# Layer 2's weight product in seven-product form, with the adjacency products between the weight products

## The chip, the cores and the metric

The kernel runs on one core of a Trainium2 chip. The metric is the device time of one execution in microseconds; the kernel before takes 1877.01 us in the median of 3 runs (1876.96 to 1878.04). Everything is computed in float32.

The engines of the core work through their own instruction streams in order and wait for each other by semaphores: TensorE (PE in the profile; PEld is its loading of the stationary operand), VectorE (DVE), ScalarE (ACT), GpSimd (POOL) and SyncE (SP), which issues most DMAs.

## What is computed

Four residual layers act on x of shape 128 x 64 x 256 (8192 rows of 256). Each takes `h = relu(layernorm(x))` and adds a graph layer of h: layer 0 two graph convolutions and four LSTM variants, layer 1 a graph convolution with two batch norms, layer 2 a product with three parts of the adjacency, layer 3 causal attention inside each graph of 64 rows. The change is in layer 2:

```python
adj_0 = jnp.diag(jnp.diagonal(adj))
adj_1 = jnp.triu(adj, k=1)
adj_2 = jnp.tril(adj, k=-1)
h = jnp.einsum('bjf,kfo->kbjo', x, W)        # W is 3 x 256 x 256
out = adj_0 @ h[0] + adj_1 @ h[1] + adj_2 @ h[2]    # per graph, then + bias
```

The last line is shortened. The kernel takes the products in the other order: first the three adjacency parts with the input, then the three weight matrices, summed.

## The kernel before

Rows are worked on in 16 supertiles of 512 rows (four quarters `q` of 128). Layers 0 and 1 come first. What matters here is the last stage, which runs from 1450 us to the end: it holds the end of layer 1, layer 2 and layer 3, in eight pairs of supertiles, an even one (`s` = 0, 2, ...) and an odd one. For each supertile, in `rest`:

- `load` fetches the residual x1 by DMA; `affine` (L1200) scales the batch-normed product of layer 1, which lies feature-major, on VectorE (on ScalarE for s = 1); `turn` (L1215) transposes it on TensorE and `turned` (L1223) adds x1 from PSUM: x2.
- `norm` (L1226) of x2 gives h2: `stats` per quarter on VectorE, `root` adds epsilon on VectorE (L1240) and takes the power -1/2 on GpSimd (L1241), `shift` makes the negative mean times root on VectorE (L1244), and `relu` (L1248) runs on ScalarE, one instruction per quarter. `biased` (L1261) adds layer 2's bias to x2 on GpSimd.
- `graphs3` (L1263) multiplies with the three adjacency parts. Each graph has 64 rows, so the stationary operand is 64 x 128, and two graphs use the two row halves of the array (64*128 in the profile). It is called four times, for each chunk `c` of 128 features and each half `k` of the rows. A call has four products and fills two PSUM banks, one copied out by ScalarE and one by VectorE (L1278), into `ag`.
- `weigh` (L1280) multiplies with the weights: for each quarter six products (two chunks by three adjacency parts), with `ag` stationary and 256 weight columns moving, 24 a supertile. `weighed` (L1288) adds x2 and gives x3.
- `norm` of x3 gives h3, which is transposed (`h3`, L1298) and copied (L1302). The attention follows: a query-key product in seven-product form (`qsum` L1313 makes the data sums on VectorE, `qproduct` L1326), the value product `hv` (L1350), `scores` (L1360), mask, maximum, exponentials on ScalarE, `turn_e` (L1381) with its copy (L1385), and `attend` (L1391), whose result is added on VectorE (L1396) and stored by DMA.

The order of the work is written by hand. Each step is put into a list with a planned time (`at(t, fn, ...)`, relative to `PERIOD * i` for pair i), the list is sorted (L1483), and each engine gets its instructions in that order. The times are only a sorting key: nothing waits for them. All PSUM banks of this stage, eight of them, come from one pool, `bank()`; a tile waits until the one that held its bank has been read. The seven-product form (Strassen's in Winograd's variant) splits both operands in 2 x 2 blocks and needs seven block products instead of eight, with sums of blocks prepared on both sides and results added up afterwards. `OF` and `weight_sum` hold its bookkeeping for the stages that already use it.

In pair i, steps of three pairs overlap: the turns and the normalization of the next pair, the weight products and queries of this one, and the last steps of the attention of the odd supertile before. The lines that set this are

```python
rest(2 * i, at, i, -8.6 if first_ else -40.2, -38.3, 0, (7.0, 12.6), 29.0, ...)
at(t_G + 0.8 * k, graphs3, ...)
at(t_W[k] + 2.6 * q, weigh, k, q)
```

where the even supertile is turned 40.2 and the odd one 27.6 before their pair's origin, and the adjacency products of the odd supertile start 3.5 after those of the even one, so that the two stand next to each other on TensorE.

Of the kernel before, what the change touches and what calls it, by code (L numbers as in the profile page):

```python
# [9 lines left out]
F32 = mybir.dt.float32  # L10
AF = mybir.ActivationFunctionType
# [9 lines left out]
def kernel(ctx: ExitStack, tc: tile.TileContext, a: dict, out: bass.AP):  # L21
# [85 lines left out]
    eps = const.tile([P, 1], F32, tag="eps", name="eps")  # L107
# [771 lines left out]
    def bn_coeffs(name, co, stats, c):  # L879
# [6 lines left out]
        nc.gpsimd.tensor_add(v, mv[:, 1:2], eps)  # L886
# [11 lines left out]
    with tc.tile_pool(name="pz", bufs=1, reuse_waits="tile") as pz:  # L898
# [238 lines left out]
        wl2 = [weight(f"wl2_{k}", a["W"][k], late) for k in range(3)]  # L1137
# [6 lines left out]

        with tc.tile_pool(name="tp", bufs=2, reuse_waits="tile") as tp_:
            tp.append(tp_)
            emit(1e9)
# [31 lines left out]

    PERIOD, HALF = 52.5, SUP // 2  # L1180
    NP = NS // 2
    with tc.tile_pool(name="pc", bufs=2, reuse_waits="tile") as pc, \
# [3 lines left out]
        def rest(s, at, only_pair, t_T, t_n, t_G, t_W, t_h, t_QH, t_S, t_soft, t_E, t_O, end):  # L1186
# [13 lines left out]
            def affine(c):  # L1200
                if s == 1:
                    nc.scalar.activation(y[c], y[c], AF.Identity, bias=co2[:, 1, c : c + 1],
                                         scale=co2[:, 0, c : c + 1])
                    return
                nc.vector.tensor_scalar(y[c], y[c], co2[:, 0, c : c + 1], co2[:, 1, c : c + 1],
                                        op0=ALU.mult, op1=ALU.add)
# [19 lines left out]
            def norm(src, tag, halves, t_rows, t_relu):  # L1226
# [11 lines left out]
                def root(qs):  # L1238
                    rn = v["rn"][:, 0, qs]
                    nc.vector.tensor_scalar_add(rn, v["mv"][:, qs, 1], EPS)  # L1240
                    nc.gpsimd.tensor_tensor(rn, rn, mhalf[:, : qs.stop - qs.start], ALU.pow)  # L1241

                def shift(qs):
                    nc.vector.scalar_tensor_tensor(v["rn"][:, 1, qs], v["mv"][:, qs, 0], -1.0,  # L1244
                                                   v["rn"][:, 0, qs], op0=ALU.mult, op1=ALU.mult)
# [5 lines left out]
                at(t_rows[0] - 0.01, new)  # L1251
                for q in range(Q):
                    at(t_rows[q // 2] + 0.6 * (q % 2), stats, q)
                for k, qs in enumerate((q2s(0), q2s(1)) if halves else (slice(0, Q),)):
                    at(t_relu[k] - 1.5, root, qs)
                    at(t_relu[k] - 0.1, shift, qs)
# [23 lines left out]
            def weigh(k, q):  # L1280
                if q == 0:
                    v["W"] = two(bank())
                for n in range(3 * KC):
                    c, m = divmod(n, 3)
                    nc.tensor.matmul(v["W"][:, q, :], v["ag"][:, c, m, ts(2 * k + q, P)],  # L1285
                                     wl2[m][:, c, :], start=(n == 0), stop=(n == 3 * KC - 1))

            def weighed(k):  # L1288
                if k == 0:
# [234 lines left out]
```

## Time and profile before

| quantity | value |
|---|---|
| median of 3 runs | 1877.01 us |
| the profiled execution | 1876.78 us, of which the span is 1875.1 us |
| granted TensorE clock | 1.00 |
| TensorE busy, whole span | 1853.9 us (99%) |
| one pair of the last stage (start to start of its adjacency products) | 50.88 us |
| engines busy from 1492 to 1545 us: DVE, ACT, POOL | 38.6, 21.4, 10.1 us |

A line of the profile in order of time reads: start, duration, engine, source line, operation, output<-inputs, shape, count. Numbers in brackets say how long the engine was idle before and what ended the wait. Instructions that follow each other are merged into one line with a count. A float32 product gives two records on TensorE. Ends of TensorE records are modelled and overlap the next start, so its rates are read from start to start. In the page's groups, a line holds the source line, the operation, shapes and count, then the busy time, the mean of one in ns, and the idle time before.

### The profile page before, as it was taken

How to read it: one execution, taken by the hardware profiler on the slowest of the kernel's cores; microseconds unless marked ns; L12 is line 12 of the kernel's file. 1: busy time of each engine (PE TensorE's matmuls, PEld its weight loads, DVE VectorE, ACT ScalarE, POOL GpSimd, SP SyncE). 2: the span in 40 equal slices, each digit the busy share in tenths (PEclk: the TensorE clock that was granted, in tenths of full speed). 3: DMA queues.
4: the chain of work that ended last, by engine and by line, in shares of the span. 5: the costliest groups of instructions: out<-in, count | busy, mean ns of one | idle time of the engine just before them, and what ended most of it. 6: DMA issues, size and time to landing. Idle time of an engine off the chain costs nothing.

```text
span 1875.1 us, 19841 instructions
## 1 busy us (share of the span) xinstructions
PE 1853.9 (99%) x7080; PEld 1168.8 (62%) x7080; DVE 1129.4 (60%) x2254; ACT 925.7 (49%) x1594; POOL 645.4 (34%) x553
## 2 busy tenths in 40 slices
PE   8999999999999999999999999999999999999999
PEld 7997444444445666666444444566444788888887
DVE  6775777634546435445633333588876776667674
ACT  6776666534435334433533333378685434433442
POOL 4451422443424433422442222267353412211220
PEclk9999999999999999999999999999999999999999
DMA  4110001000001000000000000243200111111101
GB/s 146 57 57 1 1 1 29 16 1 0 1 0 45 1 0 1 1 1 1 23 0 0 1 0 0 102 132 116 71 1 2 44 46 46 35 46 46 46 23 34
DMA packets 50642, 54.86 MB, mean 29 GB/s; under 512 B 3184, under 2 KB 45936, under 8 KB 50544
## 3 DMA queue, kind: packets, MB, share of 16 engines
q1 hardware_dynamic: 50096, 53.30, 8.9%
q8 instruction: 56, 0.92, 0.2%
q14 instruction: 42, 0.34, 0.1%
q10 hardware_dynamic: 448, 0.30, 0.0%
HBM read 36.55 MB, written 17.04 MB: 29 GB/s over the span
## 4 chain that ended last, share of the span: by engine, by line
PE 93%; DVE 3%; POOL 1%; ACT 1%; DMA 1%; issue 1%; SPq 0%; ACTq 0%; DVEq 0%; POOLq 0%
PE ps L686 34%; PE ps L692 19%; PE ps L1285 8%; PE ps L930 5%; PE ps L1047 4%; PE ps L1350 3%; PE ps L392 3%; PE ps L402 3%; PE ps L1326 2%; PE ps L431 2%; PE ps L1273 2%; PE ps L1360 2%; PE ps L1391 1%; PE ps L623 1%; PE ps L1298 1%; PE ps L579 1%
## 5 line engine op out<-in xcount | busy, mean ns | idle before, releaser
L708 DVE TENSOR_TENSOR gate<-gate,ps 128x512 f32<-128x512 f32 (+2 forms) x378 | 223.9, 620 | 449.0 <-PE ps L692 367.7
L686 PE MATMUL ps<-tx,wih 128*128 128x512 f32 (+2 forms) x996 | 441.2, 541 | 1.9 <-ACT gate L711 1.0
L686 PE MATMUL ps<-hT,wih 128*128 128x512 f32 (+2 forms) x756 | 338.5, 541 | 0.0
L711 ACT COPY gate<-ps 128x512 f32<-128x512 f32 (+2 forms) x252 | 134.5, 534 | 378.4 <-PE ps L692 325.4
L686 PEld LDWEIGHTS ps<-tx,wih 128*128 128x128 f32 x996 | 188.4, 190 | 188.2 <-issue 128.2
L704 ACT ACTIVATE gate<-gate,lbias 128x512 f32<-128x512 f32 (+2 forms) x252 | 216.7, 860 | 160.0 <-DVE gate L708 160.0
L692 PE MATMUL ps<-h,whh 128*128 128x512 f32 (+2 forms) x576 | 256.6, 527 | 0.0
L686 PEld LDWEIGHTS ps<-hT,wih 128*128 128x128 f32 x756 | 143.6, 190 | 141.6 <-issue 79.4
L692 PE MATMUL ps<-th,whh 128*128 128x512 f32 (+2 forms) x432 | 192.5, 527 | 0.0
L731 POOL TENSOR_TENSOR gate<-gate 128x1024 f32<-128x1024 f32 (+2 forms) x36 | 71.9, 2019 | 297.5 <-ACT gate L704 297.5
L1285 PE MATMUL ps<-wl,ag 128*128 128x256 f32 x768 | 172.1, 380 | 0.0
L692 PEld LDWEIGHTS ps<-h,whh 128*128 128x128 f32 x576 | 109.4, 190 | 100.2 <-issue 76.5
L1285 PEld LDWEIGHTS ps<-wl,ag 128*128 128x128 f32 x768 | 143.4, 190 | 20.2 <-ACT ag L1278 1.8
L731 POOL TENSOR_TENSOR cell<-gate 128x1024 f32<-128x1024 f32 (+2 forms) x36 | 79.4, 2225 | 174.8 <-ACT gate L704 174.8
L1241 POOL TENSOR_TENSOR ln_rn<-ln_rn,mhalf 128x4 f32<-128x4 f32 (+1 forms) x33 | 32.8, 995 | 300.8 <-DVE ln_rn L1240 300.3
L692 PEld LDWEIGHTS ps<-th,whh 128*128 128x128 f32 x432 | 82.1, 190 | 75.2 <-issue 57.4
L1248 ACT ACTIVATE h<-x,ln_rn 128x256 f32<-128x256 f32 x128 | 68.2, 593 | 103.3 <-DVE ln_rn L1244 103.3
L731 POOL TENSOR_TENSOR cell<-gate,cell 128x1024 f32<-128x1024 f32 (+2 forms) x31 | 62.8, 2044 | 110.2 <-ACT gate L704 110.2
L711 DVE COPY gate<-ps 128x512 f32<-128x512 f32 (+2 forms) x126 | 78.6, 624 | 20.8 <-PE ps L692 20.8
L704 ACT ACTIVATE gate<-ps,lbias 128x512 f32<-128x512 f32 (+2 forms) x126 | 79.6, 631 | 3.8 <-PE ps L692 1.0
L736 ACT ACTIVATE gate<-cell 128x1024 f32<-128x1024 f32 (+2 forms) x72 | 68.0, 951 | 26.1 <-POOL cell L731 26.1
L648 DVE TENSOR_TENSOR tx<-hT,tx 128x512 f32<-128x512 f32 (+2 forms) x70 | 57.7, 825 | 13.8 <-PE ps L686 10.2
(236 smaller groups left out, 2933.8 us busy)
## 6 DMA issues: line engine op xcount, KB each, us to landing
xt<-in_x_dram SPq DMA_DIRECT2D x30, 512.0 KB, 4.2
x1d<-xt SPq DMA_DIRECT2D x16, 512.0 KB, 3.0
x<-x1d SPq DMA_DIRECT2D x16, 512.0 KB, 4.9
out_dram<-x SPq DMA_DIRECT2D x15, 512.0 KB, 3.0
wih<-in_WihT_dram SPq DMA_DIRECT2D x16, 256.0 KB, 4.8
whh<-in_WhhT_dram SPq DMA_DIRECT2D x12, 256.0 KB, 4.8
xt<-in_x_dram SPq DMA_DIRECT2D x6, 128.0 KB, 3.2
wl<-in_W_dram SPq DMA_DIRECT2D x3, 256.0 KB, 3.6
```

The lines of the kernel that those rows point to most:

```text
L648: yield nc.vector.tensor_sub(t[k], *((b[1][0], b[0][0]), (b[1][1], t[0]), (b[1][1], b[1][0]), (b[0][1], t[1 % len(t)]))[k])
L686: nc.tensor.matmul(wide(p_[:, :N]), wih[0][:, OF[k], gi, :], x_, start=first_, stop=(j == 0), skip_group_check=True)
L692: nc.tensor.matmul(p_[:, :N], whh[0][:, OF[k], gi, :], h_, start=False, stop=True, skip_group_check=True)
L704: nc.scalar.activation(to, r[bank_][:, :N] if bank_ else to, fn, bias=lbias[:, l, m : m + 1])
L708: nc.vector.tensor_add(slot(n, hc), slot(n, hc), r[bank_][:, :N])
L711: op(slot(n, hc), r[bank_][:, :N])
L731: fn(*((t["G"] if isinstance(t, dict) and "G" in t else st["c"])[:, n, :, : st["N"]] for t in tiles))
L736: nc.scalar.activation(o_, c, AF.Tanh)
L930: nc.tensor.matmul(r[name], con["w1"][:, OF[j], g, :], x_, start=new, stop=(name, j) in (("a", 4), ("b", 3), ("c", 2)), skip_group_check=True)
L1047: nc.tensor.matmul(banks[name], w2[:, OF[j], k, :], x_, start=(new and k == 0), stop=(k == 1), skip_group_check=True)
L1248: nc.scalar.activation(v[tag][:, q, :], v[src][:, q, :], AF.Relu, bias=v["rn"][:, 1, q : q + 1], scale=v["rn"][:, 0, q : q + 1])
L1285: nc.tensor.matmul(v["W"][:, q, :], v["ag"][:, c, m, ts(2 * k + q, P)], wl2[m][:, c, :], start=(n == 0), stop=(n == 3 * KC - 1))
```

## The change

- Layer 2's weight product goes to the seven-product form for every supertile but the first. The blocks are two chunks of 128 features by two halves of 256 rows on the data side, and 2 x 2 blocks of 128 x 128 on the weight side, each for three adjacency parts. `ag` and its sums stay the stationary operand; 128 columns of weights or of weight sums move. A product of the form (`gproduct`) has six matmuls, two for the 128-row parts by three adjacency parts; seven of them are 42 a supertile. Data sums (`gsum`) are four GpSimd operations over 128 x 3 x 256; the weight sums are made once, on GpSimd. Results leave PSUM by seven VectorE operations (`gevict`, `gadd`) over 128 x 256. Supertile 0 uses the eight-product form with 128 moving columns (`gdirect`, 48 matmuls).
- The PSUM banks of the stage are split into three pools: one bank for the accumulation called "a", two for "b" and "c", five for all other tiles. The query products use the first two pools as well.
- The epsilon addition, the power and the shift of `root` run on GpSimd, now four operations. `qsum` moves from VectorE to GpSimd. `affine` moves to ScalarE for all supertiles but the first.
- The order changes. The even supertile is turned 14.5 before its pair's origin (40.2 before), the odd one 6.05 (27.6 before), with normalization and ReLU after that. The odd supertile's four `graphs3` calls, 1.3 apart from 7.9 on, stand between the even supertile's weight products. The seven data products of a supertile are 1.3 apart.
- The tiles of the sums and of `qk` reuse buffers of weights that are no longer needed.

```diff
-        wl2 = [weight(f"wl2_{k}", a["W"][k], late) for k in range(3)]
+        wl2 = late.tile([P, 7, 3, P], F32, tag="wl2", name="wl2")
+        for o in range(2):
+            for c in range(2):
+                nc.sync.dma_start(wl2[:, 2 * o + c], a["W"].rearrange(
+                    "m (c p) (o n) -> o c p m n", c=2, o=2)[o, c])
...
+        for k in range(4):
+            if k != 2:
+                at(B + 60 + 5.16 * k, weight_sum, wl2, k)
...
+    new_banks(a=1, bc=2, psum=5)
...
             def affine(c):
-                if s == 1:
-                    nc.scalar.activation(y[c], y[c], AF.Identity, bias=co2[:, 1, c : c + 1],
-                                         scale=co2[:, 0, c : c + 1])
+                if first_:
+                    nc.vector.tensor_scalar(y[c], y[c], co2[:, 0, c : c + 1], co2[:, 1, c : c + 1],
+                                            op0=ALU.mult, op1=ALU.add)
                     return
-                nc.vector.tensor_scalar(y[c], y[c], co2[:, 0, c : c + 1], co2[:, 1, c : c + 1],
-                                        op0=ALU.mult, op1=ALU.add)
+                nc.scalar.activation(y[c], y[c], AF.Identity, bias=co2[:, 1, c : c + 1],
+                                     scale=co2[:, 0, c : c + 1])
...
                 def root(qs):
-                    rn = v["rn"][:, 0, qs]
-                    nc.vector.tensor_scalar_add(rn, v["mv"][:, qs, 1], EPS)
-                    nc.gpsimd.tensor_tensor(rn, rn, mhalf[:, : qs.stop - qs.start], ALU.pow)
-
-                def shift(qs):
-                    nc.vector.scalar_tensor_tensor(v["rn"][:, 1, qs], v["mv"][:, qs, 0], -1.0,
-                                                   v["rn"][:, 0, qs], op0=ALU.mult, op1=ALU.mult)
+                    rn, nm = v["rn"][:, 0, qs], v["rn"][:, 1, qs]
+                    n = qs.stop - qs.start
+                    nc.gpsimd.tensor_add(rn, v["mv"][:, qs, 1], eps[:, :n])
+                    nc.gpsimd.tensor_tensor(rn, rn, mhalf[:, :n], ALU.pow)
+                    nc.gpsimd.tensor_mul(nm, v["mv"][:, qs, 0], rn)
+                    nc.gpsimd.tensor_mul(nm, nm, mone[:, :n])
...
-            def weigh(k, q):
+            def gsum(k):
+                if k == 0:
+                    v["t2"] = late.tile([P, 3 * KC, D], F32, tag="wT", name="tg")
+                t1, t2 = v["t2"][:, 0:3], v["t2"][:, 3:6]
+                if k == 0:
+                    nc.gpsimd.tensor_sub(t1, g_(0, 1), g_(0, 0))
+                elif k == 1:
+                    nc.gpsimd.tensor_sub(g_(0, 1), g_(1, 1), g_(0, 1))
+                elif k == 2:
+                    nc.gpsimd.tensor_add(t2, g_(0, 1), g_(0, 0))
+                else:
+                    nc.gpsimd.tensor_sub(g_(1, 0), g_(1, 0), t2)
+
+            def gproduct(name, j):
+                new = ("g", name) not in v
+                if new:
+                    v["g", name] = two(bank("a" if name == "a" else "bc")[:, :HALF])
...
+                for p_ in range(2):
+                    for m in range(3):
+                        nc.tensor.matmul(v["g", name][:, p_, :], x_[:, m, ts(p_, P)], wl2[:, OF[j], m, :],
+                                         start=new and p_ == m == 0,
+                                         stop=m == 2 and (name, j) in (("a", 4), ("b", 3), ("c", 2)),
+                                         skip_group_check=True)
...
-                nc.vector.tensor_add(v["x3"][:, q2s(k)], v["x2"][:, q2s(k)], v["W"])
+                nc.vector.tensor_add(w_("x3", o, n), w_("x2", o, n), v["g", name])
+
+            def gadd(o, n, name):
+                nc.vector.tensor_add(w_("x3", o, n), w_("x3", o, n), v["g", name])
...
-                nc.vector.tensor_sub(t[:, k], *(None, (b_(0, 1), b_(0, 0)), (b_(1, 1), t[:, 1]),
+                nc.gpsimd.tensor_sub(t[:, k], *(None, (b_(0, 1), b_(0, 0)), (b_(1, 1), t[:, 1]),
...
+                for t, (name, j) in zip(t_W, (("c", 2), ("a", 1), ("b", 5), ("a", 6), ("b", 3), ("a", 7), ("a", 4))):
+                    at(t, gproduct, name, j)
...
+                for t, fn, *args in ((0, gevict, 0, 0, "c"), (1, gadd, 0, 0, "a"), (2, gevict, 1, 1, "b"), (3, gevict, 0, 1, "a"),
+                                     (6, gevict, 1, 0, "a"), (4, gadd, 0, 1, "b"), (5, gadd, 1, 1, "a")):
+                    at(t_W[t] + 1.35, fn, *args)
...
-            rest(2 * i, at, i, -8.6 if first_ else -40.2, -38.3, 0, (7.0, 12.6), 29.0, 32.6, 40.0, 42.7,
+            rest(2 * i, at, i, -8.6 if first_ else -14.5, -12.5, 0,
+                 (7.0, 9.6, 12.2, 14.8) if first_ else (7.0, 8.3, 9.6, 10.9, 12.2, 13.5, 16.8),
+                 (3.3, 5.2, 7.1, 9.0), (12.5, 17.5) if first_ else (18.3, 15.3), 21.3, 24.6, 31.4, 40.0, 42.7,
...
-            rest(2 * i + 1, at, i, -3.0 if first_ else -27.6, 1.5 if first_ else -25.4, 12.3 if first_ else 3.5, (17.8, 26.5), 39.1,
+            rest(2 * i + 1, at, i, -3.0 if first_ else -6.05, 1.5 if first_ else -5.2,
+                 12.25 if first_ else 7.9, (17.85, 19.6, 20.9, 22.2, 23.5, 24.8, 27.5),
+                 (16.0, 17.9, 18.1, 22.0) if first_ else (12.3, 14.2, 16.1, 22.0), (31.4, 30.6), 35.3, 39.1,
```

## The prediction

> **What bounds the kernel now.** I read the page's busy table first, then TensorE alone in order of time, then all engines over one pair of supertiles.
>
> ```profile
> PE 1853.9 (99%) x7080; PEld 1168.8 (62%) x7080; DVE 1129.4 (60%) x2254; ACT 925.7 (49%) x1594; POOL 645.4 (34%) x553
> L1285 PE MATMUL ps<-wl,ag 128*128 128x256 f32 x768 | 172.1, 380 | 0.0
> ```
>
> TensorE is busy 99% of the span. The second line is the product that the change rewrites: 768 records are 16 supertiles of 24 products, two records to an f32 product. A busy share can hide waits, so I take TensorE from start to start, in the view in order of time:
>
> ```profile
> 1509.18 1.95 PE L1360 MATMUL ps<-h3T,qk 128*128 128x128 f32 x16
> 1510.96 1.89 PE L1391 MATMUL ps<-hw,eT 128*128 128x256 f32 x8
> 1512.79 5.47 PE L1273 MATMUL ps<-adj,h 64*128 64x192 f32 x64
> 1518.19 5.45 PE L1285 MATMUL ps<-wl,ag 128*128 128x256 f32 x24
> 1523.47 0.60 PE L1381 MATMUL ps<-ident,sc 128*128 128x128 f32 x4
> ...
> 1829.21 10.53 PE L1285 MATMUL ps<-wl,ag 128*128 128x256 f32 x48
> 1839.57 1.89 PE L1391 MATMUL ps<-hw,eT 128*128 128x256 f32 x8
> ```
>
> 48 records of 256 columns take 10.36 us: 0.216 each. 16 records of 128 columns, each with its own stationary, take 1.78: 0.111 each. The 64 adjacency records (L1273; two 64-row tiles side by side) take 5.40. ScalarE's copies of their groups of eight start every 0.65 us, which is 0.081 a record and 5.20 for 64. The excess sits at the edges: the eight L1391 records before them take 1.83 where 8 x 0.216 is 1.73, the last adjacency record runs out 0.20 late, and the 24 records after them take 5.28 where 24 x 0.216 is 5.18. **One block of adjacency products costs 0.40 us at its two edges.** L1273 starts again at 1563.67, 1614.55, and on to 1818.09, always 50.88 apart. My sum of one pair from these rates is 50.68; the other 0.2 is a wait for ReLU before L1298. So the pair has almost no slack in TensorE, and the order of its instructions decides what else may show.
>
> The other engines' durations come from the same view of all engines:
>
> ```profile
> 1564.62 0.48 ACT L1278 COPY ag<-ps 128x384 f32<-128x384 f32 x1 [4.21 <-PE ps L1273]
> 1576.26 1.28 DVE L1224 TENSOR_TENSOR x<-x,ps 128x512 f32<-128x512 f32 x2
> 1577.45 0.42 DVE L1235 BATCH_NORM_STATS2 ln_st<-x 128x6 f32<-128x256 f32 x1
> ...
> 1581.84 1.02 POOL L1241 TENSOR_TENSOR ln_rn<-ln_rn,mhalf 128x4 f32<-128x4 f32 x1 [26.78 <-DVE ln_rn L1240]
> 1582.89 0.16 DVE L1244 SCALAR_TENSOR_TENSOR ln_rn<-ln_mv,ln_rn 128x4 f32<-128x4 f32 x1 [0.60 <-POOL ln_rn L1241]
> ...
> 1583.09 2.08 ACT L1248 ACTIVATE h<-x,ln_rn 128x256 f32<-128x256 f32 x4 [10.58 <-DVE ln_rn L1244]
> ```
>
> Eviction 0.60 from start to start, statistics 0.53 per quarter, power 1.02, four ReLUs 2.08, adjacency copy 0.48. VectorE starts 0.2 after TensorE's end, a copy of L1273 0.27.
>
> **What the Trainium skill says.** "TensorEngine Tiling (Array Packing)", Key Properties: changing the tiling mode drains TensorE; the 0.40 us a block agrees. "TensorE: Matmul & The Clock Gate", Back-to-back issue gap and LDWEIGHTS: the spacing in a stream is set by the weight load and the matmul together, the load by its columns. The trace agrees that a load of 128 columns still hides behind 128 moving columns (0.111 against half of 0.216). "GPSIMD Engine Reference", Key points: GpSimd contends with VectorE instructions that read two SBUF tensors. Here L1313 took 0.42 alone and 0.94 beside L1261. "Perfetto Trace Analysis" on GpSimd says to trust spacing rather than spans, so for its small operations I take the spacing of the chain L888, L889, L890: 0.27.
>
> **The change, part by part, for a steady pair.**
>
> 1. Weight product: 24 x 2 x 0.216 = 10.36 becomes 42 x 2 x 0.111 = 9.33 per supertile: -1.03, over 15 supertiles -15.4. Supertile 0 goes direct in 48 products of 128 columns: 10.66, +0.3.
>
> 2. Adjacency products between weight products: before, the 64 records of a pair are one block. In the changed order the even supertile's 32 are a block and the odd one's four groups of eight are each a block between weight products: five blocks, four more edges, +1.6 a pair in pairs 1 to 7, +11.2. Pair 0 has three blocks in both. The gain of 1 is 2.06 a pair, so 0.46 remains.
>
> 3. Turns, normalization and ReLU of the next pair, which stood up to 40 us ahead of its adjacency products, now stand just before them. This is the step that I expect to hurt. Count from the end of the odd supertile's last turn transpose. TensorE runs on: three products 1.30, score transposes 0.44, scores 1.78, attention 1.73, edge 0.10, two adjacency groups 1.30: it wants the third group of the even supertile at 6.65. VectorE: start 0.2, second eviction done near 1.0, three statistics 1.6, the copy of the score transposes (0.7, ahead of the fourth in VectorE's order), the fourth 0.53 and its tail: 3.94. GpSimd: a hop of 0.12, add 0.27, power 1.09, two multiplies 0.46: 5.88. ScalarE's order is odd ReLU, ReLU, ReLU, then the even supertile's first adjacency copy. Three ReLUs from 5.95 end at 7.42, the copy at 7.90. The third group needs the bank that this copy frees, for only five banks are left to everything but the products (one pool of eight before). So it starts at 7.95; the fourth needs the second copy, which stands behind the fourth ReLU: 8.82, end 9.47, against 7.95 unhindered. **Stall 1.5 us a pair, 7 pairs: +10.5.** A place, not a rate: it is there only if the chain is late by more than the reach. Below nothing it can't go; if the hops are shorter than I read it is 1.0, if VectorE is held up 2.2.
>
> 4. One bank for the accumulation "a": each eviction must read it before the next product of "a" may add. Between the sixth and seventh product of the even supertile only 0.44 of transposes lie, against 0.2 + 0.42 + 0.05 for VectorE's add: +0.23 a pair. The other waits of this kind have 1.3 us of cover. Pair 0 has none in this place: +0.65.
>
> 5. Data sums on GpSimd, four of 128x768 per supertile. The trace has no such row; it has these:
>
> ```profile
> L731 POOL TENSOR_TENSOR gate<-gate 128x1024 f32<-128x1024 f32 x20 | 46.6, 2351 | 184.3 <-ACT gate L704 184.3
> L423 POOL TENSOR_TENSOR t<-g 128x256 f32<-128x256 f32 x30 | 21.9, 731 | 71.3 <-ACT g L396 71.3
> ```
>
> A line through them gives 1.81 at 768 (bounds 1.5, of two 128x384 passes without start cost, and 2.35). Eight make 14.5 a pair; with query sums (8 x 0.73), bias (8 x 0.74), and four roots (4 x 1.82) GpSimd has 33.5 of 52 us, from 11. On the path: in the frame of 3 the first sum starts at 9.0 behind the biases, the third ends at 14.6, TensorE asks for it near 17. The odd third ends at 24.9, needed at 28. Hidden with 2 to 3 us to spare; without that cover each late microsecond counts whole.
>
> 6. Off VectorE: scaling (0.53 each, 0.80 on ScalarE, issued 17 us early), query sums, root add and shift. Seven evictions of 0.42 replace two of 0.68. VectorE goes from 37.5 to about 32 us a pair and loses its contending operations: nothing on the path. The root on GpSimd alone is 1.82 against 0.17 + 1.02 + 0.16 with hops, about +0.3 in each chain, already in step 3. Before the odd h3 transposes the chain (evict, attention, statistics 2.1, root 1.8, ReLU 2.1) is 8.4 against 8.3 of TensorE: +0.1 where 0.2 was. In the last pair no turn fills in: +0.9.
>
> 7. Pair 0: its wait of 0.8 for L1302 goes, one of about 1.2 for GpSimd's crowded roots (weight sums, biases) comes; with its own 1.0 from step 1, 0.3 lost on supertile 0, 0.65 from step 4, 0.5 for banks at the start, and 1.8 of idle there unchanged, my walk through its order ends 0.8 early. Four loads of weights instead of three, and three GpSimd weight sums of about 1 us in the stage before, have tens of us until use: nothing.
>
> Sum: pair 0 -0.8; pairs 1 to 6 each -2.06 + 1.6 + 1.5 + 0.23 - 0.1 = +1.2, +7.0; pair 7 -2.06 + 1.6 + 1.5 + 0.23 + 0.9 = +2.2. Together +8.4 on the profiled 1876.78 (span 1875.1, 1.7 outside it), which is 0.2 under the median 1877.01: **1885**.
>
> **Rivals.** *The ReLU chain arrives in time* (not slower): step 3 vanishes if the odd ReLU starts 1.5 us earlier than my sum has it; a bit less than half of it must vanish for the slowdown to fall under 0.2%. For it: 1.3 us of eight small operations with hops are my reading. Against: every duration is a row of the trace. 1885 - 10.5 = 1874.5.
> *Edges cost nothing beside short products as well* (faster): with both 10.5 and 11.2 gone, 1863. Against it: three blocks of different length show the same 0.4.
> *GpSimd becomes the bound*: above about 2.3 us per 768-wide sum its cover is gone and the root behind the odd sums holds h3; one us a pair, 1892.
> *The product doesn't shrink*: loads of 128 columns showing beside 128 moving ones would give 42 x 2 x 0.19 = 16.0 by the load's own span, +11 a pair; the 0.111 of L1360 rules it out.
>
> **How the numbers follow.** No change means within 0.2%, 3.75 us, about what a measurement can tell. My case has 0.50 (1881 to 1890), GpSimd 0.13, the chain in time 0.20 (1871 to 1879), both gone 0.17. Slower 0.50 + 0.13 + 0.02, same 0.16, faster 0.17 + 0.02. From 1869 to 1892 leaves 0.13 below and 0.06 above.
>
> **What would show it.** In the changed trace: weight products of 128 columns at 0.111 from start to start; four short adjacency blocks between them, each with 0.4 of edges; a TensorE gap of 1 to 2 us inside the even supertile's 32 adjacency records, released by ScalarE's copy; pairs 52 us apart; GpSimd near 33 us of a pair, 768-wide sums near 1.8. Pairs under 50.5 apart would make me wrong.

## The result and the profile after

The changed kernel takes 1888.39 us in the median of four runs (1887.98 to 1889.16), the kernel before 1876.99 us beside it (1876.65 to 1878.04): a ratio of 1.006, 95% interval 1.0043 to 1.0078. It is slower by 11.4 us. The prediction said 1885.0 us (1869 to 1892), with 0.65 for slower. The profiled execution took 1887.99 us, its span 1886.2 us, 11.1 more than before, at the same granted clock of 1.00.

The page's busy table and the group of the rewritten product (engine, busy time, share, instructions; then line, shapes, count, busy, mean ns of one, idle before):

```profile
PE 1857.4 (98%) x7668; PEld 1176.9 (62%) x7668; DVE 1094.8 (58%) x2175; ACT 943.9 (50%) x1622; POOL 815.9 (43%) x777
L1314 PE MATMUL ps<-wl,ag 128*128 128x128 f32 x900 | 111.9, 278 | 1.9 <-POOL ag L1300 1.2
```

TensorE's share fell from 99% to 98%, although it has more instructions: it waits now. Products are named below by their number in the form; in order of time a supertile's seven are the second, first, fifth, sixth, third, seventh and fourth, of which the first, sixth, seventh and fourth go to the accumulation "a". Where TensorE waits is seen in the view of TensorE in order of time over one pair (start, duration, line, tiles, shape, count; in brackets the idle time before and its releaser):

```profile
1618.07 1.57 PE L1281 MATMUL ps<-adj,h 64*128 64x192 f32 x16
1620.53 1.79 PE L1281 MATMUL ps<-adj,h 64*128 64x192 f32 x16 [0.89 <-ACT ag L1286]
1622.25 1.60 PE L1314 MATMUL ps<-wl,ag 128*128 128x128 f32 x12
1623.78 0.92 PE L1281 MATMUL ps<-adj,h 64*128 64x192 f32 x8
1624.63 1.60 PE L1314 MATMUL ps<-wl,ag 128*128 128x128 f32 x12
...
1634.57 0.60 PE L1432 MATMUL ps<-ident,sc 128*128 128x128 f32 x4
1635.34 4.25 PE L1314 MATMUL ps<-wl,ag 128*128 128x128 f32 x36 [0.17 <-POOL ag L1300]
1639.43 2.84 PE L1314 MATMUL ps<-wl,tg 128*128 128x128 f32 x24
1642.11 1.50 PE L1314 MATMUL ps<-wl,ag 128*128 128x128 f32 x12
...
1670.31 1.57 PE L1281 MATMUL ps<-adj,h 64*128 64x192 f32 x16
```

Pairs are 52.24 apart (1618.07 to 1670.31), 50.88 before: +1.36. From start to start: the even supertile's 32 adjacency records take 4.18 (1618.07 to 1622.25). Four groups at 0.65 and the 0.20 at the end are 2.80, so 1.38 is a wait: 1.16 where the third group begins (1619.37 to 1620.53), 0.22 behind it. A product of the form takes 1.53 between two adjacency blocks (1622.25 to 1623.78) and 1.34 elsewhere (1642.11 to 1643.45); a block of eight records takes 0.85 where 0.65 would be eight of 0.081. That is 0.20 in the block and 0.20 in the products beside it, 0.40 a block. The score transposes (1634.57) take 0.77 to the next start where four take 0.44: 0.33 of wait.

The span's 11.1 us, from the starts of the adjacency blocks: pair 0 begins 0.58 earlier (1460.88 against 1461.46) and lasts 52.70 against 51.33, +0.8 in sum; six pairs of +1.36 are +8.2; from the last pair's start to the end it is 59.17 against 57.01, +2.2.

Below, "apart" is always the distance between two pairs' adjacency blocks in the steady part.

### The profile page after: what moved, and what is told of

Same layout as the page of the kernel before. It is cut to its first block, busy times and chain, and to the rows that moved or that the text cites. A ratio compares the mean times of both kernels' runs of the same rounds, so it can differ in the third digit from the quotient of the medians.

```text
span 1886.2 us, 21316 instructions
## 1 busy us (share of the span) xinstructions
PE 1857.4 (98%) x7668; PEld 1176.9 (62%) x7668; DVE 1094.8 (58%) x2175; ACT 943.9 (50%) x1622; POOL 815.9 (43%) x777
## 4 chain that ended last, share of the span: by engine, by line
PE 85%; POOL 7%; DVE 4%; ACT 2%; issue 1%; DMA 0%; POOLq 0%; DVEq 0%; ACTq 0%
PE ps L688 34%; PE ps L694 19%; PE ps L932 5%; PE ps L1049 4%; PE ps L1314 4%; PE ps L394 3%; PE ps L404 3%; PE ps L1401 2%; PE ps L433 2%; PE ps L1377 2%; POOL ag L1300 1%; PE ps L625 1%; POOL tg L1298 1%; ACT h L1257 1%; PE ps L1411 1%
## 5 line engine op out<-in xcount | busy, mean ns | idle before, releaser
L1314 PE MATMUL ps<-wl,ag 128*128 128x128 f32 x900 | 111.9, 278 | 1.9 <-POOL ag L1300 1.2
L1314 PEld LDWEIGHTS ps<-wl,ag 128*128 128x128 f32 x900 | 104.7, 192 | 9.3 <-issue 5.4
L1286 DVE COPY ag<-ps 128x384 f32<-128x384 f32 x64 | 35.5, 555 | 57.7 <-PE ps L1281 57.4
L1381 ACT COPY qk<-ps 128x256 f32<-128x256 f32 x60 | 22.1, 369 | 88.5 <-PE ps L1377 69.3
```

What stands on the lines that cost most here:

```text
L1314: nc.tensor.matmul(v["g", name][:, p_, :], x_[:, m, ts(p_, P)], wl2[:, OF[j], m, :], start=new and p_ == m == 0, stop=m == 2 and (name, j) ...
```

## The experiments

The theory in the prediction: the product gains 2.06 a pair on TensorE, and three things take back more than that, the edges of adjacency blocks (1.6), the late normalization chain in front of them (1.5), and a single bank for the accumulation "a" (0.23). The rivals: too few banks, GpSimd at its bound, or a product that doesn't gain. The first four runs take these apart one at a time, the next four ask what else can take their place, and the last four try to collect the gain. Four of the twelve expectations were met (the late ReLUs, the one block, the exchanged products, and pair 0 in the part that its edit touches). Most misses have one form: a cost was gone as expected, and another wait stood in its place.

### The odd ReLUs behind the even adjacency copies

```diff
-t_n + (4.1 if s == 1 else 3.8 if s % 2 else 7.5)
+t_n + (4.1 if s == 1 else 7.9 if s % 2 else 7.5)
```

> The odd supertile's four ReLUs stand behind the even supertile's four adjacency copies on ScalarE; nothing else of the chain is shortened. My theory: the 1.4 us gap inside the even supertile's adjacency products comes from the first copy standing behind three late ReLUs, so the gap nearly goes, and the first odd adjacency group waits about 0.3 us instead: about 1.0 less a pair, 7 pairs, 1881 us (1879 to 1884), pairs about 51.2 apart. Rival, too few PSUM banks: the third group has to wait for a copy whatever stands before it, the gap keeps 1 us or more, 1887 to 1889.

Measured: 1882.93 us, ratio 1.0031 (1.0019 to 1.0042). Pairs are 51.44 apart, 0.80 less than in the changed kernel. What changed is ScalarE's order. ScalarE in the changed kernel:

```profile
1618.53 1.58 ACT L1257 ACTIVATE h<-x,ln_rn 128x256 f32<-128x256 f32 x3 [2.83 <-POOL ln_rn L1254]
1620.02 0.46 ACT L1286 COPY ag<-ps 128x384 f32<-128x384 f32 x1
1620.38 0.60 ACT L1257 ACTIVATE h<-x,ln_rn 128x256 f32<-128x256 f32 x1
```

Three ReLUs that wait for GpSimd's root, then the copy of the first adjacency group, which TensorE has finished near 1618.8, then the third group at 1620.53. With the edit, ScalarE and then TensorE:

```profile
1617.98 0.48 ACT L1286 COPY ag<-ps 128x384 f32<-128x384 f32 x1 [3.33 <-PE ps L1281]
...
1617.03 3.30 PE L1281 MATMUL ps<-adj,h 64*128 64x192 f32 x32
1620.43 1.57 PE L1314 MATMUL ps<-wl,ag 128*128 128x128 f32 x12
```

The 32 records run in one piece, 3.40 from start to start. So 0.78 of the stall comes from the late ReLU ahead of the copy on ScalarE, and goes with no bank added. The 0.6 that remain over 2.80 are VectorE's: its copies stand behind the second half of the attention's addition there, and the one that the first product reads ends at 1620.38, 0.05 before the product starts.

### The odd adjacency groups next to the even ones

```diff
-                 12.25 if first_ else 7.9, ...
+                 12.25 if first_ else 3.2, ...
-at(t_G + (1.8 if s == 1 else 1.3 if s % 2 else 0.8) * k, graphs3, ...
+at(t_G + (1.8 if s == 1 else 0.8) * k, graphs3, ...
```

> The odd supertile's four adjacency calls stand directly behind the even one's, as in the kernel before, so that a pair has one block of them instead of five. My theory, 0.40 us for the two edges of each block: 1.6 less a pair, 7 pairs, 1877 us (1876 to 1880, the upper end if five banks slow the long block), with the gap of 1.4 still in it. Rival, edges cost nothing and the short blocks only show waits for data: no gain, 1887 to 1890.

Measured: 1878.51 us, ratio 1.0008 (0.9999 to 1.0016). Pairs are 50.82 apart, 1.42 less, where four edges of 0.40 are 1.6. TensorE:

```profile
1564.35 1.57 PE L1281 MATMUL ps<-adj,h 64*128 64x192 f32 x16
1566.81 4.56 PE L1281 MATMUL ps<-adj,h 64*128 64x192 f32 x48 [0.89 <-ACT ag L1286]
1571.30 2.94 PE L1314 MATMUL ps<-wl,ag 128*128 128x128 f32 x24
```

The wait of 0.89 is still there, and the time is back within the uncertainty of the kernel before: the split blocks and the late chain are two separate costs. The block takes 6.95 to the next start, 0.17 more than 5.40 for its records and its end and 1.38 for the wait. So the edges gave back the 1.6, and 0.17 of it went into a longer wait inside the block. The Trainium skill, "TensorEngine Tiling (Array Packing)", Key Properties, says that changing the mode drains TensorE; this run doesn't show the drain itself, but agrees with a price of about 0.40 for each block between products.

### The odd turn and its chain earlier

```diff
-rest(2 * i + 1, at, i, -3.0 if first_ else -6.05, 1.5 if first_ else -5.2,
+rest(2 * i + 1, at, i, -3.0 if first_ else -11.4, 1.5 if first_ else -9.6,
```

(ReLU, bias and scaling keep their places.)

> The odd supertile's turn and statistics stand some 4 to 5 us earlier in the order (behind the even supertile's scores instead of inside the odd one's query products); ScalarE's order of ReLUs and adjacency copies stays. My theory, the ReLU chain is late: the ReLUs end before the first copy is due, the gap of 1.4 us goes, 1879 us (1877 to 1882), pairs about 51.0 apart. Rival, too few PSUM banks or the order on ScalarE by itself: the gap stays, 1887 to 1889.

Measured: 1891.53 us, ratio 1.0076 (1.006 to 1.0093): a miss, 3 us above the changed kernel, with pairs 52.67 apart. TensorE and VectorE:

```profile
1612.74 1.03 PE L1401 MATMUL ps<-wvo,h3T 128*128 128x256 f32 x4
1614.77 0.67 PE L1377 MATMUL ps<-tq,aqk 128*128 128x256 f32 x2 [0.99 <-DVE qk L1384]
...
1620.18 3.31 PE L1281 MATMUL ps<-adj,h 64*128 64x192 f32 x32
```

```profile
1612.32 0.39 DVE L1384 TENSOR_TENSOR qk<-qk,ps 128x256 f32<-128x256 f32 x1
1612.62 0.42 DVE L1245 BATCH_NORM_STATS2 ln_st<-x 128x6 f32<-128x256 f32 x1
...
1614.23 0.72 DVE L1384 TENSOR_TENSOR qk<-qk,ps 128x256 f32<-128x256 f32 x2
```

The 32 records take 3.41, so as much of the stall is gone as in the first run. But the turn's statistics now stand on VectorE ahead of the query additions (L1384), and the last query product waits 1.17 for its bank (1613.60 to 1614.77). The chain can't simply be moved: VectorE is idle for two fifths of a pair, and full where the chain would have to go.

### One data sum done twice

```diff
-                    nc.gpsimd.tensor_add(t2, g_(0, 1), g_(0, 0))
+                    for _ in range(2):
+                        nc.gpsimd.tensor_add(t2, g_(0, 1), g_(0, 0))
```

> The third data sum of each supertile is made twice, one more GpSimd operation of 128x768 (1.8 us), 3.6 us more GpSimd work a pair. My theory, GpSimd is hidden with 2 us or more to spare, and only the root of the even supertile's h3 behind the odd sums comes near: 0 to 0.7 more a pair, 1888 to 1894. Rival, GpSimd already sets the pace: 3.6 more a pair, 1913 or above.

Measured: 1899.19 us, ratio 1.0116 (1.0101 to 1.0131), pairs 53.47 apart: +1.23 for 3.6 us of added GpSimd work a pair. About two thirds of it are hidden, so GpSimd is not the bound; but in these places 2.4 of 3.6 us is all that was covered. The loss shows at the even h3 transposes, whose root stands behind the odd sums on GpSimd:

```profile
1595.58 0.48 PE L1350 MATMUL ps<-ident,h 128*128 128x128 f32 x2
...
1597.31 1.50 PE L1315 MATMUL ps<-wl,ag 128*128 128x128 f32 x12
```

1.73 from 1595.58 to 1597.31, where the changed kernel has 0.88 (1591.21 to 1592.09): 0.85 of the 1.23. Another 0.38 is at the odd products that read the sums, 3.06 for 24 records instead of 2.68. The expectation counted too much cover.

### Six banks for the other tiles, one for "b" and "c"

```diff
-    new_banks(a=1, bc=2, psum=5)
+    new_banks(a=1, bc=1, psum=6)
```

> The changed kernel with six banks for everything but the products and one for the accumulations b and c together (two before). My theory has two parts in the stall inside the even supertile's 32 adjacency records, the late copy and the lack of a bank for the third group: with a sixth bank the third group starts at once and only the fourth waits for the first copy, so the stall shrinks by about 0.65 us a pair: 1883.5 us (1881.5 to 1886). If banks count for nothing there and the late ReLU itself (the products of the second half need nothing new from it) sets the stall: 1888 (1887 to 1889.5). If one bank for b and c makes its own wait: above 1889.

Measured: 1926.06 us, ratio 1.0259 (1.0244 to 1.0275), pairs 56.15 apart where the granted clock is 1.00. Three of the six steady pairs are 57.8 apart: in them the clock is 0.97 on average, from 1609.5 to 1612.8 for instance 0.52. The run tells two things. TensorE:

```profile
1621.92 1.10 PE L1377 MATMUL ps<-tq,aqk 128*128 128x256 f32 x4 [1.60 <-POOL ln_rn L1253]
...
1631.66 1.89 PE L1281 MATMUL ps<-adj,h 64*128 64x192 f32 x18
1634.11 1.78 PE L1281 MATMUL ps<-adj,h 64*128 64x192 f32 x14 [0.56 <-ACT ag L1286]
1635.82 1.60 PE L1314 MATMUL ps<-wl,ag 128*128 128x128 f32 x12
```

First, the sixth bank lets one more product (two records) start, and the 32 records still take 4.16 (4.18 with five). One bank more is worth nothing while ScalarE's first copy ends as late as it does (1634.06 here). Second, with one bank for "b" and "c" the query products wait for VectorE to read "c", 1.77 here. The profile names GpSimd's L1253 as the releaser. The addition of "c" on VectorE started at 1621.36, behind four statistics, a mask and a maximum, and took 0.41, so it ended 0.15 before TensorE went on.

### The roots' small operations back on VectorE

The diff of the change, undone in `root` and `shift`.

> The changed kernel with the root's epsilon addition and shift back on VectorE as before the change (only the power on GpSimd). My sum has the root at about 0.3 us more in each chain when it is on GpSimd alone: the stall shrinks by 0.3 us a pair, 1886.2 us (1884 to 1887.5). Rival, the shift on VectorE waits for the power and holds VectorE's evictions behind it: no gain or a loss, 1888 to 1892.

Measured: 1894.49 us, ratio 1.0095 (1.008 to 1.011), pairs 53.07 apart, +0.83. The gain that I expected is there, and twice as large: the even adjacency block takes 3.60 instead of 4.18. The rival's loss is larger. VectorE:

```profile
1603.74 0.16 DVE L1250 TENSOR_SCALAR ln_rn<-ln_mv 128x4 f32<-128x4 f32 x1
1605.03 0.16 DVE L1254 SCALAR_TENSOR_TENSOR ln_rn<-ln_mv,ln_rn 128x4 f32<-128x4 f32 x1 [1.12 <-POOL ln_rn L1251]
1605.11 0.75 DVE L1386 TENSOR_TENSOR qk<-qk,ps 128x256 f32<-128x256 f32 x2
```

The shift waits 1.12 for the power, and the query additions behind it on VectorE wait with it. TensorE then shows a wait of 0.43 at the last query product, 0.73 at the odd supertile's scores, whose query copy on ScalarE stands behind a ReLU that waits for a shift, and 0.26 within its products. So the root on GpSimd is a gain in this order, though each root is longer there.

### Two of the seven products exchanged

```diff
-(7.0, 8.3, 9.6, 10.9, 12.2, 13.5, 16.8),
+(7.0, 8.3, 9.6, 10.9, 13.5, 12.2, 16.8),
```

The product for "a" that came sixth in time now comes fifth, ahead of one for "b". In this kernel it is also issued just ahead of the eviction of "a" before it, so that this eviction takes a sum with one product too many; the amount of work on each engine is the same.

> The changed kernel with the even supertile's sixth and fifth-to-last products exchanged, so that a full product of b lies between the seventh product of a and its last one. This takes step 4's wait away (0.23 by my sum, 0.33 in the trace after) and no other: pairs 52.24 to 51.95 apart, 1886.2 us (1885 to 1887.2). If the wait is GpSimd's sum, as the profile's name for the releaser has it, it stays: 1888.4.

Measured: 1885.28 us, ratio 1.0046 (1.0031 to 1.0061), pairs 51.82 apart: -0.42 where 0.33 was asked for. TensorE:

```profile
1634.33 0.60 PE L1432 MATMUL ps<-ident,sc 128*128 128x128 f32 x4
1634.77 4.18 PE L1314 MATMUL ps<-wl,ag 128*128 128x128 f32 x36
```

0.44 from the transposes to the product, without a wait. GpSimd's sums are untouched, so its name in the brackets of the changed kernel was wrong (in the first two runs the brackets at this place name VectorE's L1342): VectorE's addition for the seventh product ended there at 1635.19, 0.15 before TensorE went on. Step 4 is confirmed. The three products behind it also take 4.02 to the next start (1634.77 to 1638.79), where they took 4.09 behind the wait: 0.07 more of the 0.42.

### The seven-product form in the order of the kernel before

Four kernels put the turns back behind the even supertile's seventh product and make all 64 adjacency records one block again. The first of them has the single bank for "b" and "c" as well; in it the eviction of the sixth product takes one product too many again. ReLU, bias and scaling of the turned rows move along in all four.

```diff
-rest(2 * i, at, i, -8.6 if first_ else -14.5, -12.5, 0,
+rest(2 * i, at, i, -8.6 if first_ else -40.2, -32.5, 0,
...
-rest(2 * i + 1, at, i, -3.0 if first_ else -6.05, 1.5 if first_ else -5.2,
-     12.25 if first_ else 7.9, ...
+rest(2 * i + 1, at, i, -3.0 if first_ else -27.6, 1.5 if first_ else -25.4,
+     12.25 if first_ else 3.5, ...
```

> The seven-product form alone, in the order of the kernel before: the turns of both supertiles and their normalization stand far ahead of their adjacency products again, all 64 adjacency records of a pair are one block, the last but one product of the accumulation a comes one turn earlier, the pools of banks are one, one and six. My sum by its own steps: pair spacing 50.88 of before, less 2.06 of step 1, plus some 0.2 for waits of the h3 transposes: 49.0 (48.8 to 49.4). With pair 0 at +0.8 and the last pair at +0.9 as the changed kernel has them, 1865.5 us (1863 to 1869), below both kernels. Rival, the product itself is worth less than its sum beside 128-column stationaries and sums on GpSimd: pairs near 50.9 and 1877 or more. Rival, GpSimd is near its bound, so that its root behind the odd sums holds the even h3: an own wait of 0.5 to 1 us a pair at the h3 transposes, pairs 49.6 to 50, 1869 to 1873.

Measured: 1920.57 us, ratio 1.024 (1.0223 to 1.0257). Pairs are 55.7 to 55.9 apart where the granted clock is 1.00, and 57.35 in the half of them where it is 0.97 on average. TensorE's waits from 1490 to 1860 us (line, releaser, sum, times, longest) show that most of the miss is waits, and not the product's rate (24 records take 2.68 here too):

```profile
PE ps L1314 <- DVE x L1342: 20.3, 13, 2.6
PE ps L1377 <- DVE qk L1384: 16.7, 13, 2.6
```

Both are for VectorE: the second as in the run with six banks, the first comes where the turns' additions stand ahead of the additions that read "a". The next kernel goes back to pools of one, two and five banks, with the turns behind the seventh product's result:

```diff
-rest(2 * i, at, i, -8.6 if first_ else -14.5, -12.5, 0,
+rest(2 * i, at, i, -8.6 if first_ else -37.64, -32.5, 0,
...
-rest(2 * i + 1, at, i, -3.0 if first_ else -6.05, 1.5 if first_ else -5.2,
+rest(2 * i + 1, at, i, -3.0 if first_ else -26.3, 1.5 if first_ else -19.5,
```

> The seven-product form in the order of the kernel before, now with the changed kernel's pools of banks (one, two, five). Both turns stand right behind the seventh product of a weight product, so they lie between it and the last product of a, and VectorE's addition for the seventh product stands ahead of the turns' additions; the normalization of the turned rows has its time in stretches where VectorE has little else; all 64 adjacency records are one block. By my sum the edges (1.6), the stall (1.4) and the wait of step 4 (0.33) are gone and the product's gain of 2.06 stays: pairs 52.24 - 3.3 = 48.9 apart, with 0.1 to 0.5 for five banks under one block of eight groups: 49.2 (48.9 to 49.6), 1888.4 - 7 x 3.0 = 1867 us (1864 to 1871). Rival, five banks pace a block of eight groups by the copies: another 0.8 a pair, 1873. Rival, the early turns cost VectorE or GpSimd a wait that they don't cost the product with its eight results to add: above 1877.

Measured: 1880.47 us, ratio 1.002 (1.0013 to 1.0027), pairs 51.36 apart: a miss by 13 us. Edges, stall and step 4's wait are gone, but again VectorE's order takes over: the odd query additions stand behind the statistics of the turned rows (1.17), the eviction of the fourth product behind the even turn's additions (0.49), one block of eight groups on five banks takes 5.90 where eight banks gave 5.40, and the odd supertile's sixth product is 0.33 late. The third kernel moves the first two out of the way, and gives each half of a turn a result tile of its own, so that its addition can stand later:

```diff
-    at(t_T + 0.1 * k + 0.01, turned, k)
+    at(t_T + 0.1 * k + (0.01 if s < 2 or s % 2 else 4.2), turned, k)
...
-rest(2 * i + 1, at, i, -3.0 if first_ else -26.3, 1.5 if first_ else -19.5,
+rest(2 * i + 1, at, i, -3.0 if first_ else -26.3, 1.5 if first_ else -16.0,
```

> The run before in the order of the kernel before left two waits of its own, both for VectorE's order: 1.17 a pair where the odd supertile's query additions stood behind the statistics of the turned rows, and 0.49 where the eviction of the last product of a stood behind the even turn's additions. Here the odd statistics stand behind the last query addition, and the even turn's additions behind that eviction and the first statistics of x3. Pairs 51.36 - 1.66 = 49.7 apart (49.4 to 50.2), 1880.5 - 7 x 1.66 = 1869 us (1866 to 1873), below the kernel before. Rival, VectorE's work is only shifted and another instruction is late by as much (the h3 statistics behind the turn's additions): pairs above 50.6, 1875 or more.

Measured: 1878.12 us, ratio 1.0007 (0.9999 to 1.0016), pairs 50.93 apart, level with the kernel before; the rival in its expectation is what happened. TensorE:

```profile
1616.08 5.97 PE L1281 MATMUL ps<-adj,h 64*128 64x192 f32 x64
1621.99 2.94 PE L1314 MATMUL ps<-wl,ag 128*128 128x128 f32 x24
...
1635.46 1.50 PE L1314 MATMUL ps<-wl,tg 128*128 128x128 f32 x12
1637.64 1.58 PE L1314 MATMUL ps<-wl,tg 128*128 128x128 f32 x12 [0.68 <-DVE x L1342]
...
1653.02 0.42 PE L1349 MATMUL ps<-ident,h 128*128 128x128 f32 x2
1653.60 0.33 PE L1349 MATMUL ps<-ident,h 128*128 128x128 f32 x1 [0.16 <-ACT h L1257]
1654.10 0.77 PE L1349 MATMUL ps<-ident,h 128*128 128x128 f32 x5 [0.16 <-ACT h L1257]
1654.70 1.95 PE L1411 MATMUL ps<-h3T,qk 128*128 128x128 f32 x16
```

The block takes 5.91, 0.5 over the kernel before. The odd supertile's sixth product, the fourth in time, starts 0.84 late (2.18 for a product of 1.34), because VectorE's addition for "a" stands behind the turn's additions and statistics. The odd h3 transposes take 1.68 where 0.87 is their own, 0.6 more than the wait that the kernel before had. Their chain from the eviction of the fourth product to the ReLU is as long as in the changed kernel (6.09 in both), but the odd turn's transposes (0.87) no longer stand ahead of them. Together 1.95, against the 1.97 that the product measures below. So the product's gain is there, and this order spends it on three waits that the kernel before did not have.

### Two adjacency blocks

```diff
-                 12.25 if first_ else 7.9, ...
+                 12.25 if first_ else 12.26, ...
-(7.0, 8.3, 9.6, 10.9, 12.2, 13.5, 16.8),
+(7.0, 8.3, 9.6, 10.9, 13.4, 12.6, 16.8),
```

(with the odd groups 0.08 apart and the odd ReLUs late, as in the first run)

> The changed kernel with the odd supertile's ReLUs behind the even adjacency copies, its four adjacency groups as one block between the sixth and seventh product of the even supertile, and the fifth product of the form exchanged with the seventh of a behind it. Gone: the stall (1.38), three blocks' edges (1.2), the wait of step 4 (0.33), 2.9 in all. Come: the even h3 asks for its root some 2.4 us earlier while GpSimd's sums start only 1.4 earlier, so a wait of about 0.5 to 1 at the h3 transposes if GpSimd's cover is as small as doubling one sum showed. Pairs 49.9 apart (49.3 to 50.6), 1888.4 - 7 x 2.35 = 1872 us (1868 to 1877). If GpSimd is not near its bound: 1868. If the block of odd groups waits for the odd ReLUs all the same: above 1877.

Measured: 1881.49 us, ratio 1.0024 (1.0015 to 1.0034), pairs 51.24 apart. The largest part of the miss is a wait for GpSimd, but not where the expectation had it. TensorE, then GpSimd:

```profile
1622.76 1.50 PE L1314 MATMUL ps<-wl,tg 128*128 128x128 f32 x12
1625.20 1.60 PE L1314 MATMUL ps<-wl,tg 128*128 128x128 f32 x12 [0.94 <-POOL tg L1302]
```

```profile
1619.54 1.82 POOL L1298 TENSOR_TENSOR tg<-ag 128x768 f32<-128x768 f32 x1 [2.51 <-ACT ag L1286]
1621.43 1.83 POOL L1300 TENSOR_TENSOR ag<-ag 128x768 f32<-128x768 f32 x1
1623.34 1.81 POOL L1302 TENSOR_TENSOR tg<-ag 128x768 f32<-128x768 f32 x1
```

Three sums in a row, from the last copy on, end at 1625.15; TensorE has the three products before them done at 1624.10 and waits 1.10. In the changed kernel the adjacency blocks between the products, with their edges, are what covers these sums: the third ended at 1627.02 and was asked for at 1629.41. Taking the edges away uncovers them. Another 0.6 of the even block's wait stays, as in the first run.

### Pair 0

```diff
-at(t_G + (1.8 if s == 1 else 0.8) * k, graphs3, ...
+at(t_G + (0.6 if s == 1 else 0.8) * k, graphs3, ...
```

(on top of the last kernel in the order of the kernel before)

> The same, and in pair 0 the four adjacency groups of supertile 1 stand 0.6 instead of 1.8 apart, so that all are ahead of supertile 0's last quarter of direct products. In pair 0 the sums on GpSimd then don't wait for the last group's copy: the wait of 0.52 of the sixth product and one edge of 0.40 go, up to 0.3 comes for five banks under four groups at once: 0.6 less than the run beside it (0.2 to 0.9), all within pair 0. If pair 0's loss comes from GpSimd's own queue of small work, nothing changes.

Measured: 1876.66 us, ratio 1.0 (0.9991 to 1.0009): level with the kernel before, and the fastest version of the seven-product form. Pair 0 lasts 52.05 (1460.77 to 1512.82) instead of 52.95, -0.90; the rest of the difference between the two, 0.6, is an earlier start of the stage, which the edit doesn't touch. In the changed kernel GpSimd has time there, and waits for the copies of adjacency groups that stand behind supertile 0's direct products:

```profile
1476.15 1.81 POOL L1298 TENSOR_TENSOR tg<-ag 128x768 f32<-128x768 f32 x1 [2.08 <-DVE ag L1286]
1477.92 1.00 POOL L311 TENSOR_TENSOR wl<-wl 128x384 f32<-128x384 f32 x1
1480.03 1.82 POOL L1300 TENSOR_TENSOR ag<-ag 128x768 f32<-128x768 f32 x1 [1.11 <-DVE ag L1286]
```

No version tried is faster than the kernel before.

## Why the prediction was right, point by point

The side was right, the size 3.4 us short (1885.0 against 1888.39), and in the steady pairs the mechanisms were the ones named. About 1.6 us of the shortfall is pair 0, most of the rest is small errors in the terms of the steady pair.

| step | predicted, us a pair | measured |
|---|---|---|
| 1, product | -2.06 | -1.97 (2.68 for 24 records) |
| 2, four more edges | +1.6 | +1.57 in the trace, 1.42 when undone |
| 3, late chain | +1.5 | +1.38, of which 0.80 go with the ReLU alone |
| 4, one bank "a" | +0.23 | +0.33 and 0.07 behind it, 0.42 when undone |
| 6, odd h3 | -0.1 | -0.05 (transposes 0.93 where they took 1.08, the scores behind them 0.10 longer) |
| a pair | +1.2 | +1.36 |
| pair 0 | -0.8 | +0.8 |
| last pair with the tail | +2.2 | +2.2 |

Step 1. 24 records take 2.68, so 84 take 9.38 against 9.33 predicted, twice a pair, where the products took 20.73 before without their edge. The rival of a product that doesn't shrink is out. No run shows the full gain as time, but the third kernel in the old order accounts for it to within 0.1 (less 1.97, plus 1.95, measured +0.05).

Step 2. Right, and the largest term that an edit of the order alone gives back. The rival of edges that cost nothing beside short products is out.

Step 3. The place, the releaser and the size were right. One part of the reason, "for only five banks are left", is not shown: with six the block was as long. A group fills two banks, so a sixth lets only its first product start; whether seven or eight would hide the late copy was not tried. The first rival, the chain arriving in time, fell with the 0.89 in the trace; and moving the chain earlier shortened the stall by 0.77 but cost a new wait of 1.17 on VectorE.

Step 4. Right in place and cause, short by 0.1 to 0.2: VectorE's addition ends 0.15 before TensorE goes on, where the sum had 0.05. The name that the profile gives the releaser would have led elsewhere.

Step 5. The 768-wide sums take 1.81 to 1.83, as read off a line through two other shapes; GpSimd is busy 31.98 of 52.24 where 33.5 was said. "2 to 3 us to spare" was right: the even third sum ends 2.4 before it is asked for (1627.02, 1629.41), and 3.6 us of added sums cost 1.23. GpSimd as the bound is out for the changed order; in the tighter order of the two blocks it was the largest wait.

Step 6. VectorE is busy 32.08 a pair where about 32 was predicted. "Nothing on the path" was right, and understated: undoing the root's move alone costs 0.83 a pair, since VectorE would wait for the power with the query additions behind it. The prediction priced only the longer chain.

Step 7 is the step that failed: pair 0 is 0.8 later instead of 0.8 earlier. Its own terms don't give its result. A wait of 0.8 that goes and 1.0 from step 1 stand against 1.2 for GpSimd, 0.3 on supertile 0, 0.65 from step 4 and 0.5 for banks, which is 0.85 later. Whether a sign was lost, or the walk had a gain that the text doesn't name, can't be told from it. That 0.85 is so near the measured 0.79 is in part luck: the stage starts 0.58 earlier, which no term has, and pair 0 itself lasts 1.37 longer.

The wait put down to "GpSimd's crowded roots" is there, but GpSimd stands idle twice in the stretch (2.08 and 1.11 in the view above), for copies of adjacency groups placed behind direct products. Behind that the sixth product is 0.67 late and the even h3 transposes are 0.86 late. A second late product belongs to step 4, which had 0.65 for it. The two products on TensorE:

```profile
1483.78 1.60 PE L1314 MATMUL ps<-wl,tg 128*128 128x128 f32 x12 [0.52 <-POOL tg L1302]
1490.41 1.57 PE L1314 MATMUL ps<-wl,ag 128*128 128x128 f32 x12 [0.61 <-POOL tq L1364]
```

The fourth product, at 1490.41, starts 0.77 late. It doesn't read `tq`, the tile that the brackets name; VectorE's addition for the seventh product (L1342, from 1489.85 on, 0.42 long) ended 0.14 before it. Placing the groups earlier gave 0.90 back in the older order; in the changed order itself that was not tried.

What stays open: the terms measured for a pair add up to +1.33 of the 1.36. The moves of the scaling to ScalarE and of the query sums to GpSimd were not undone by themselves. And whether a seven-product version below the kernel before exists isn't settled: in the older order the remaining waits are for VectorE, for banks and for the h3 chain, and taking two of them away made another longer and brought a new one.

## What to carry to other kernels

A product with fewer multiplications moves its cost to results and operands: here seven instead of two reads of PSUM a supertile, in order, on an engine that the page shows 58% busy, and sums on one that it shows 43% busy. Before trading, lay out these engines' queues at the places where TensorE will ask, because in a kernel whose main engine is at 99% the order there decides, and a saved microsecond uncovers the next wait. When undoing one cost, ask what it was covering: the block edges, dear as they were, gave GpSimd the time for its sums, and the turn's transposes gave the h3 chain its time.

## What the runs showed of the hardware

- VectorE's additions of a result in PSUM took 0.42 beside GpSimd's 768-wide sums as well as without them (at 1633.43 beside a sum from 1633.52 on, at 1643.65 with GpSimd idle, both in the changed kernel). The slowing from 0.42 to 0.94 that the prediction read for an operation with two operands in SBUF does not show here.
- In three places the releaser in brackets was not the one that counted: GpSimd's L1300 and L1364 (changed kernel) and L1253 (six banks) stood for a VectorE addition that ended 0.14 to 0.15 before TensorE went on.
- An edge between the two tilings costs the same beside products with 128 and with 256 moving columns: 0.40 a block in the traces of both kernels.
- In the two kernels with the longest TensorE waits the granted clock fell to about half in single stretches: 0.52 from 1609.5 to 1612.8 (six banks), 0.50 from 1612.5 to 1615.7 (first kernel in the old order). A pair with such a stretch is 1.7 longer (57.84 against 56.15, 57.35 against 55.67). Other pairs have the same waits and run at 1.00, so what sets it off is not shown.
